# A graph layer whose first tiles come row by row from ScalarE's queue in seven groups, with a new setup order and a new end

## The chip, the cores and the metric

One NeuronCore of a Trainium2 chip runs the whole kernel. The metric is the device time of one execution in microseconds (us), the median over several executions: 2478.72 us over 9 runs, which lie between 2464.89 and 2493.82 us. The engines are named PE (TensorE; PEld is its weight load), DVE (VectorE), ACT (ScalarE), POOL (GpSimd) and SP (SyncE, which here only issues DMAs). A DMA issued by ACT is in ACT's own instruction order.

## The reference

A message-passing layer over N = 6250 nodes and E = 200000 edges, followed by a residual sum and a layer norm. The edges come sorted by destination; the sources are random.

```
w    = silu(edge_attr @ W1 + b1) @ W2 + b2              # E x 9, from E x 32
msg  = einsum('ef,em,fmg->eg', x[src], edge_sh * w, W_tp)   # F = 64, M = 9
agg  = segment_sum(msg, dst, N) / sqrt(16)
emb  = silu(node_vec[:, None] @ Wn1 + bn1) @ Wn2 + bn2
gamma, beta = split(emb, 2)
y    = layernorm(x + agg * (1 + gamma) + beta)
```

## The kernel before

**Tiling.** A tile is 128 edges, a group is KB = 16 tiles, and there are NBLK = 98 groups (the last, group 97, has 11 tiles). Because edges are sorted, all edges of a tile fall into a window of 8 consecutive nodes (a general path for other data stands behind the loop and is not taken here). The order of the instructions on each engine is the order of the code: the schedule is written out by hand, and each engine takes its instructions in that order and waits by semaphores.

**Rows of x.** Each tile needs the rows x[src], 128 x 64, in `hs`. There are three ways to get them. The first is `gather` (L89): POOL issues one indirect DMA per tile (L91) into the group's buffer of the pool `gath`, which has seven buffers; it works six groups ahead (AHEAD). The second is `pick` (L463): the last `picked(g)` tiles of a group (3 or 4, Q = 4) are selected out of a copy of x that lies in SBUF, `xs`, by one-hot matrices `hot_k`. One pick is 14 matmuls of 448 columns (seven slices h, high and low part of x) into one of two px buffers, then two DVE operations: `xm` (L484) masks the sum and L486 reduces it into `hs`. There are 355 picks. The third is `load_rows` (L98): in 16 groups (SPG: 7, 13, 19 and so on) tile 0 is not gathered; SP loads its 128 row numbers into registers, eight at a time (L101), and issues one small DMA per row (L106), 22 rows per step (SPR) over the six steps before the group's turn.

**One step of the loop (L603, i = 0 to 97)**, in order: the gathers of group i+6; the loads (`load` L367 of the edge features, `near` L378, `load_keys` L388, `gate_load` L344); `load_rows` on SP; `keys(i+2)` (L451: ACT copies the keys kr to a PSUM tile pk); the first pick of group i+1, with the matmuls of `nodes` (L582) and the first two `hots` (L456, one-hots on DVE) between its matmuls; the other hots; `hidden(i+2)` (L398: the first edge layer, then Silu on ACT into `st`, L411); `second(i+1)` (L415: the second layer, then ACT adds the bias into `p2s`, L423); `windows(i)` (L494); in odd steps `project` (L530); the second pick, with `weights` (L425: transposes of p2s and the DVE products that end in `a`, L442) and in odd steps `turn` (L548) between its matmuls; the other picks.

`windows` is the main product: for each tile a matmul (L504) of the group's hs with `a` into a tile pz, eight tiles to a pz, then four ACT copies (L514) per half into `zt`. Its first matmul waits for all gathers of the group (L509). `project` multiplies zt with W_tp (L543), and ACT copies the result to `rt` (L546). `turn` transposes it, and `halves` (L520) splits it in a high part (ACT, L524) and a low part (DVE, L525) and makes one-hots on DVE (L528). `place` (L554) adds these rows up by node (L559); ACT copies the part that goes on to the next pair (`carry`, L565), DVE adds (yt, L568), `bring` (L572) turns the sums, and `finish_nodes` (L667) does the layer norm and issues the store from SP (L684).

**Setup (L134).** SP loads src, w1 (L140), the edge features, w2 and dst; ACT's queue carries dst's first row, node_vec, b1 and then x in three parts (L155). POOL makes index vectors and begins the gathers of groups 0 to 5. DVE computes the keys of all picked rows (L209 to L217); PE transposes them, ACT copies, SP writes them to DRAM (`kd`) and `load_keys` brings them back, spread over all partitions. x is split into xs: per slice ACT copies twice (L292, L293) and DVE subtracts (L294), and `between` (L261) puts small products in between. `base` (L239) spreads dst's first row over the partitions with matmuls of one row (p_b, L242) and subtracts it (rel, L243). Then come the picks of group 0. The load of xb is issued at L318.

**End (L639 to L657).** In the last step the product of the last pair of full groups follows the picks, then windows(96) and windows(97), project, place, bring and the last store run one after the other.

The few lines that decide which tiles are gathered and picked:

```
def picked(g):                                                        # L50
    return Q - (3 * g % 8 < 3)
for t in range(g * KB + (g in SPG), g * KB + tiles(g) - picked(g))    # L94, gather
```

Of the kernel before, what the change touches and what calls it, by code (L numbers as in the profile page):

```python
# [15 lines left out]
P = 128  # L16
# [15 lines left out]
SPR = 22  # L32
EPS = 1e-5
# [16 lines left out]
def picked(g):  # L50

    return Q - (3 * g % 8 < 3)
# [7 lines left out]
def gnn_resnorm_kernel(ctx: ExitStack, tc: tile.TileContext, x, src, dst, dst_row, ea, sh, cn,  # L60
# [18 lines left out]
    with ExitStack() as fast:  # L79
# [9 lines left out]
        def gather(g):  # L89
# [4 lines left out]
                for t in range(g * KB + (g in SPG), g * KB + tiles(g) - picked(g))]  # L94

        src_r = keep.tile([len(SPG), P], I32)

        def load_rows(g, e0):  # L98
            for e in range(e0, min(e0 + SPR, P), 8):
                n = min(8, min(e0 + SPR, P) - e)  # L100
                _, vs = nc.values_load_multi_w_load_instructions(  # L101
                    src_r[SPG.index(g):SPG.index(g) + 1, e:e + n], engines=[mybir.EngineType.SP],
                    min_val=0, max_val=NPAD - 1,
                    skip_runtime_bounds_check_because="src is below N, as for the gathers")
                for k in range(n):
                    nc.sync.dma_start(hs[g][e + k:e + k + 1, 0, :], x[bass.ds(vs[k], 1), :])  # L106
# [27 lines left out]
        def setup(temp):  # L134
# [4 lines left out]
            for q in range(4):  # L139
                nc.sync.dma_start(w1bd[q * D:(q + 1) * D, (q % 2) * H:(q % 2 + 1) * H], w1)  # L140
            nc.sync.dma_start(src_i[:, AHEAD * KB:], src[:, AHEAD * KB:])
            xb_r = xb.rearrange("p j f -> p (j f)")
            row_i = xb_r[0:1, 0:NBLK * KB].bitcast(I32)
            nc.scalar.dma_start(row_i, dst[0:1, :])
            first_i = temp.tile([NBLK, KB], I32)
            nc.scalar.dma_start(first_i, dst[0].rearrange("(g k) -> g k", k=KB))
            cn_j = temp.tile([NJ, P], F32)
            nc.scalar.dma_start(cn_j, cn)
            for s in range(2):
                nc.scalar.dma_start(b1c[s * H:(s + 1) * H, :], b1.unsqueeze(1))  # L150
# [3 lines left out]
            for h0, h1 in ((0, 2), (2, 4), (4, 7)):  # L154
                nc.scalar.dma_start(xk[:, h0:h1, :], x_v[:, h0:h1, :])  # L155
            load(0)
            for s in range(2):
                nc.sync.dma_start(w2p[s * H:(s + 1) * H, s * M:(s + 1) * M], w2)
            nc.sync.dma_start(dst_i, dst)
# [14 lines left out]
            one = temp.tile([1, 1], F32)  # L174
            nc.vector.memset(one, 0.0)
            one_o = temp.tile([1, 1], F32)
            nc.scalar.activation(one_o, one, AF.Silu)
            row_f = xb_r[0:1, NBLK * KB:2 * NBLK * KB]
            nc.scalar.copy(row_f, row_i)
            first_t = temp.tile([NBLK, KB], F32)  # L180
            nc.scalar.copy(first_t, first_i)
# [5 lines left out]
            nc.vector.tensor_add(ident2, ident[:, 0:F], ident[:, F:P])  # L187
            zero = temp.tile([P, 1], F32)
            nc.vector.memset(zero, 0.0)
            for k in range(2):  # L190
                nc.vector.memset(ht[k][H:H + 1], 1.0)
            nc.vector.memset(wtc2[F:P, 4], 0.0)
            ones1 = temp.tile([1, P], F32)
            nc.vector.memset(ones1, 1.0)
            nc.vector.memset(eps, EPS)
            nc.vector.tensor_copy(nk, nk_i)
            nc.vector.tensor_copy(wi, n_i[:, 0:W])
            nc.vector.tensor_copy(li, n_i[:, 0:J])


            zt_r = zt.rearrange("p a c k w -> p (a c k w)")
            s_f, kp, kh, rest, t0, t1 = [zt_r[:, k * C:(k + 1) * C] for k in range(6)]
            ti = [t.bitcast(I32) for t in (t0, t1)]
            s_f = s_f.rearrange("p (g k) -> p g k", k=Q)
            nc.vector.tensor_copy(s_f[:, 0:NBLK - 1, :],
                                  src_i.rearrange("p (g k) -> p g k", k=KB)[:, 0:NBLK - 1, KB - Q:])
# [652 lines left out]
```

## Time and profile before

| what | value |
|---|---|
| median of 9 runs | 2478.72 us |
| the profiled execution's own time | 2489.51 us |
| its span, first to last instruction | 2487.6 us |
| mean granted TensorE clock in it | 0.818 |
| instructions | 34363 |
| bytes moved by DMA, mean rate | 96.16 MB, 39 GB/s |
| hot_k on DVE (L460) | 355, 1080 ns each, 370.3 us |
| zt copies on ACT (L514) | 784, 272 ns each, 213.6 us |
| matmuls of the picks (L475) | 4970, 409 ns each by the profile |

The profile is of one execution, taken by the hardware profiler. In a row of groups stand the source line, the engine, the operation, output<-input, the shapes, the number of instructions, and then the busy time and the mean of one; behind the second bar stand the idle time before them on their engine and what ended it ("issue": nothing the profile shows). In a row of the timeline stand the start in us, the duration, the engine, the line and the operation; x32 means that so many instructions in a row are shown together, and a bracket holds the wait before it and what ended it. SPq is the queue of SP. The waits of an engine's DMA queue are listed with the total time, the number and the longest.

### The profile page before, as it was taken

The numbers are of one execution on the slowest core, as the hardware profiler recorded it, in microseconds if no ns is written. First come the engines' busy times: TensorE is split into PE (matmuls) and PEld (weight loads), VectorE is DVE, ScalarE is ACT, GpSimd is POOL, SyncE is SP. The second block draws the span as 40 slices with busy tenths as digits, with TensorE's granted clock in tenths as the row PEclk, the third lists the DMA queues.
The fourth block names the chain that finished last, engine by engine and source line by source line (L and its number), as shares of the span: only waits on it lengthen the run. The fifth ranks groups of instructions, "written<-read, shape, count | busy, mean of one in ns | idle before, by whom it ended". The sixth has DMA issues, their size and how long they took to land.

```text
span 2487.6 us, 34363 instructions
## 1 busy us (share of the span) xinstructions
PE 1662.5 (67%) x10810; PEld 1345.6 (54%) x10810; DVE 1142.5 (46%) x1987; ACT 529.2 (21%) x1335; POOL 1128.4 (45%) x1201
## 2 busy tenths in 40 slices
PE   3077576767667577676776686667675766767697
PEld 1055464655556456555555565545564655556576
DVE  3045354544444454444544454445344535444475
ACT  2012122212122122121212121212121212212132
POOL 7634444444534454445354544544444445455400
PEclk7588787888878888888787887878888888888898
DMA  4121111111111111111111111111111111111110
GB/s 115 32 50 44 23 43 36 38 35 45 40 31 35 43 37 38 33 46 36 36 36 41 36 37 33 44 31 37 33 43 35 34 45 35 36 35 46 37 32 5
DMA packets 90940, 96.16 MB, mean 39 GB/s; under 512 B 37162, under 2 KB 51452, under 8 KB 90749
## 3 DMA queue, kind: packets, MB, share of 16 engines
q0 software_dynamic: 38144, 39.14, 8.2%
q1 hardware_dynamic: 51842, 53.09, 7.4%
q8 instruction: 88, 1.44, 0.2%
q10 hardware_dynamic: 762, 1.64, 0.2%
q14 instruction: 104, 0.84, 0.1%
HBM read 92.04 MB, written 1.73 MB: 38 GB/s over the span
## 4 chain that ended last, share of the span: by engine, by line
PE 44%; another core or an unknown queue 28%; DVE 14%; issue 11%; ACT 3%; POOL 0%; DVEq 0%; DMA 0%; POOLq 0%; ACTq 0%
PE px L475 29%; PE pz L504 4%; DVE xm L484 4%; PE p L403 3%; PE pt L543 3%; PE p L420 2%; DVE hs L486 2%; DVE a L442 2%; DVE hot_k L460 2%; PE p L430 1%; DVE c L528 1%; PE ps L559 1%; DVE p L436 1%; ACT st L411 1%
## 5 line engine op out<-in xcount | busy, mean ns | idle before, releaser
L91 POOL DMA_INDIRECT hs<-in_x_dram,src_i x1192 | 1127.1, 946 | 1244.3 <-PE pz L504 893.3
L475 PE MATMUL px<-xs,hot_k 128*128 128x448 f32 x4970 | 1264.2, 409 | 515.5 <-DVE xm L484 432.8
L475 PEld LDWEIGHTS px<-xs,hot_k 128*128 128x128 f32 x4970 | 1001.0, 212 | 648.7 <-DVE xm L484 458.3
L484 DVE SCALAR_TENSOR_TENSOR xm<-li,jl,px 128x448 f32<-128x448 f32 x355 | 240.1, 676 | 877.3 <-remote 628.5
L460 DVE TENSOR_TENSOR hot_k<-pk,nk 128x896 fp32r<-128x896 f32 x355 | 370.3, 1080 | 2.7 <-issue 2.7
L411 ACT ACTIVATE st<-p,b1c 128x1024 f32<-128x1024 f32 x98 | 109.5, 1117 | 630.3 <-PE p L403 506.6
L486 DVE TENSOR_REDUCE hs<-xm 128x64 f32<-128x448 f32 x355 | 220.0, 620 | 12.2
L514 ACT COPY zt<-pz 64x160 f32<-64x160 f32 (+2 forms) x784 | 213.6, 272 | 28.7 <-PE pz L504 20.0
L420 PE MATMUL p<-st,w2p 128*32 128x256 f32 x784 | 77.6, 445 | 164.9 <-DVE xb L356 108.7
L504 PEld LDWEIGHTS pz<-a,hs 128*64 128x64 f32 x3126 | 127.9, 160 | 49.8 <-issue 48.8
L420 PEld LDWEIGHTS p<-st,w2p 128*32 128x32 f32 x784 | 18.3, 115 | 244.1 <-issue 144.7
L504 PE MATMUL pz<-a,hs 128*64 128x72 f32 x3126 | 143.9, 255 | 0.5 <-issue 0.5
L442 DVE TENSOR_TENSOR a<-oh,p 128x1152 f32<-128x1152 f32 x98 | 132.6, 1353 | 3.3
L436 DVE TENSOR_TENSOR p<-p,sh 128x72 f32<-128x72 f32 x196 | 47.1, 240 | 173.9 <-issue 124.0
L565 ACT COPY carry<-ps 128x128 f32<-128x128 f32 x48 | 12.8, 267 | 490.5 <-PE ps L559 412.2
L403 PE MATMUL p<-ea,w1bd 64*128 64x512 f32 x392 | 114.3, 660 | 0.0
L525 DVE TENSOR_TENSOR r<-pt,r 128x128 fp32r<-128x128 f32 (+1 forms) x50 | 14.4, 288 | 165.8 <-issue 90.3
L543 PE MATMUL pt<-zt,wtc 128*64 128x128 f32 x960 | 75.9, 315 | 17.4 <-ACT st L411 15.7
L680 ACT ACTIVATE var<-var,eps 128x2 f32<-128x2 f32 (+1 forms) x25 | 7.4, 295 | 365.0 <-DVE var L679 365.0
L524 ACT CAST r<-pt 128x128 fp32r<-128x128 f32 (+1 forms) x50 | 13.2, 264 | 328.6 <-remote 247.4
L543 PEld LDWEIGHTS pt<-zt,wtc 128*64 128x64 f32 x960 | 65.6, 164 | 19.5 <-ACT st L411 17.6
L430 PE MATMUL p<-ident,p2s 128*128 128x128 f32 x196 | 54.9, 281 | 18.3 <-issue 18.2
(122 smaller groups left out, 619.9 us busy)
## 6 DMA issues: line engine op xcount, KB each, us to landing
hs<-in_x_dram SPq DMA_DIRECT2D x2048, 0.2 KB
ea<-in_ea_dram SPq DMA_DIRECT2D x49, 512.0 KB
hs<-in_x_dram,src_i POOLq DMA_INDIRECT x1192
kr<-kd SPq DMA_DIRECT2D x49, 256.0 KB
sh<-in_sh_dram SPq DMA_DIRECT2D x49, 144.0 KB
cb<-cn_d SPq DMA_DIRECT2D x12, 128.0 KB
out_dram<-o SPq DMA_DIRECT2D x24, 64.0 KB
gam<-in_x_dram ACTq DMA_DIRECT2D x2, 448.0 KB
```

The source lines that it names most:

```text
L91: hs_dma[g] = [nc.gpsimd.indirect_dma_start(out=hs[g][:, t - g * KB, :], out_offset=None, in_=x, in_offset=bass.IndirectOffsetOnAxis(ap=sr ...
L403: nc.tensor.matmul(p1[:, i, :], w1bd[i * 64:(i + 1) * 64, :], e[i * 64:(i + 1) * 64, :], start=True, stop=True)
L411: nc.scalar.activation(st[g], p1_t.pop(g), AF.Silu, bias=b1c)
L420: nc.tensor.matmul(p2[g][c * D:(c + 1) * D, 0, :].rearrange("p (i e) -> p i e", i=2), w2p, s[:, :, c * P:(c + 1) * P], start=True, stop=True)
L442: nc.vector.tensor_mul(a[g], oh_t.pop(g)[:, :, None, :].to_broadcast([P, KB, M, W]), sw.unsqueeze(3).to_broadcast([P, KB, M, W]))
L460: nc.vector.tensor_tensor(hot_k[g, t], pk_t[g][:, t, None, :].to_broadcast([P, J, P]), nk.unsqueeze(2).to_broadcast([P, J, P]), op=ALU.is_ ...
L475: nc.tensor.matmul(px.rearrange("p f l -> p (f l)"), hot_k[g, t][:, h, :], xs[i][:, h].rearrange("p f l -> p (f l)"), start=(h == 0 and i ...
L484: nc.vector.scalar_tensor_tensor(xm, li[:, None, :].to_broadcast([P, F, J]), jl[:, c:c + 1], px, op0=ALU.is_equal, op1=ALU.mult)
L486: nc.vector.tensor_reduce(hs[g][:, tiles(g) - q + t, :], xm, AX.X, ALU.add)
L504: mm = nc.tensor.matmul(pz[v * F:(v + 1) * F, k // 2].rearrange("p m w -> p (m w)"), hsg[:, k0 + k, :], ag[:, k0 + k].rearrange("p m w -> ...
L514: nc.scalar.copy(z[h * F:(h + 1) * F, 0:5 - h, k0 + v:k0 + n:2, :].rearrange("p m k w -> p k m w"), pz[v * F:(v + 1) * F, 0:(n + 1 - v) // ...
L543: nc.tensor.matmul(pt[h * F:(h + 1) * F, 0, 0:P], wtc2[:, c, :], z[h][:, c], start=(c == 0), stop=(c == 4))
```

## The change

Rows: seven groups (ACG: 16, 28 and so on to 88) get tile 0 row by row from ACT's queue, 11 rows per step (ACR) over twelve steps, into two buffers of their own (`hs_r`). The issues stand in the step after `windows`, `project` and `gate_hidden` and before the second pick. Group 97 has three picks instead of four, so there are 354 picks and 1186 gathers.

Setup: x goes first in ACT's queue, in four parts; the small loads move to SP; the keys of groups 0 and 1 are spread over the partitions by matmuls of ones with a scaled identity (`keys_first`), those of the other groups go through DRAM as before but later (`keys_rest`); x is split with one ACT copy per slice; dst's first row is spread by a broadcast DMA instead of `base`; hidden, second and weights of group 0 stand among its picks, and most of the constants come after them.

End: windows(96) comes inside step 96, ahead of the picks of group 97, project(48) and place stand among these, windows(97) takes its halves in reverse, with a px buffer beside each pz buffer, and DVE does half of its zt copies. Stores go out at the start of the next step.

```diff
@@ -30,6 +30,8 @@
 J = 7
 SPG = range(7, NBLK, 6)
 SPR = 22
+ACG = range(16, NBLK, 12)
+ACR = 11
...
-    return Q - (3 * g % 8 < 3)
+    return Q - (3 * g % 8 < 3 or g == NBLK - 1)
...
-                for t in range(g * KB + (g in SPG), g * KB + tiles(g) - picked(g))]
-        src_r = keep.tile([len(SPG), P], I32)
+                for t in range(g * KB + (g in SPG or g in ACG), g * KB + tiles(g) - picked(g))]
+        src_r = keep.tile([len(SPG) + len(ACG), P], I32)
+        row_g = list(SPG) + list(ACG)
+        hs_r = [keep.tile([P, F], F32, name=f"hs_r{k}") for k in range(2)]
         def load_rows(g, e0):
-            for e in range(e0, min(e0 + SPR, P), 8):
-                n = min(8, min(e0 + SPR, P) - e)
+            q = row_g.index(g)
+            if g in SPG:
+                eng, kind, n1, to = nc.sync, mybir.EngineType.SP, SPR, hs[g][:, 0, :]
+            else:
+                eng, kind, n1, to = nc.scalar, mybir.EngineType.Activation, ACR, hs_r[ACG.index(g) % 2]
+            for e in range(e0, min(e0 + n1, P), 8):
+                n = min(8, min(e0 + n1, P) - e)
                 _, vs = nc.values_load_multi_w_load_instructions(
-                    src_r[SPG.index(g):SPG.index(g) + 1, e:e + n], engines=[mybir.EngineType.SP],
+                    src_r[q:q + 1, e:e + n], engines=[kind],
                     min_val=0, max_val=NPAD - 1,
                     skip_runtime_bounds_check_because="src is below N, as for the gathers")
                 for k in range(n):
-                    nc.sync.dma_start(hs[g][e + k:e + k + 1, 0, :], x[bass.ds(vs[k], 1), :])
+                    eng.dma_start(to[e + k:e + k + 1, :], x[bass.ds(vs[k], 1), :])
...
             nc.sync.dma_start(src_i[:, 0:AHEAD * KB], src[:, 0:AHEAD * KB])
+            xk = gam.rearrange("p (h l) f -> p h (l f)", h=J)
+            x_v = x.rearrange("(p h l) f -> p h (l f)", h=J, l=J)
+            for h0, h1 in ((0, 1), (1, 2), (2, 4), (4, 7)):
+                nc.scalar.dma_start(xk[:, h0:h1, :], x_v[:, h0:h1, :])
             for q in range(4):
                 nc.sync.dma_start(w1bd[q * D:(q + 1) * D, (q % 2) * H:(q % 2 + 1) * H], w1)
-            nc.sync.dma_start(src_i[:, AHEAD * KB:], src[:, AHEAD * KB:])
-            xb_r = xb.rearrange("p j f -> p (j f)")
-            row_i = xb_r[0:1, 0:NBLK * KB].bitcast(I32)
-            nc.scalar.dma_start(row_i, dst[0:1, :])
-            first_i = temp.tile([NBLK, KB], I32)
-            nc.scalar.dma_start(first_i, dst[0].rearrange("(g k) -> g k", k=KB))
-            cn_j = temp.tile([NJ, P], F32)
-            nc.scalar.dma_start(cn_j, cn)
+            row_i = xb.rearrange("p j f -> p (j f)")[:, 0:NBLK * KB].bitcast(I32)
+            load(0, split=True)
+            nc.sync.dma_start(dst_i[:, 0:2 * KB], dst[:, 0:2 * KB])
+            nc.sync.dma_start(row_i[:, 0:2 * KB], rows(dst[0, 0:2 * KB], P))
             for s in range(2):
-                nc.scalar.dma_start(b1c[s * H:(s + 1) * H, :], b1.unsqueeze(1))
-            xk = gam.rearrange("p (h l) f -> p h (l f)", h=J)
-            x_v = x.rearrange("(p h l) f -> p h (l f)", h=J, l=J)
-            for h0, h1 in ((0, 2), (2, 4), (4, 7)):
-                nc.scalar.dma_start(xk[:, h0:h1, :], x_v[:, h0:h1, :])
-            load(0)
+                nc.sync.dma_start(b1c[s * H:(s + 1) * H, :], b1.unsqueeze(1))
             for s in range(2):
                 nc.sync.dma_start(w2p[s * H:(s + 1) * H, s * M:(s + 1) * M], w2)
-            nc.sync.dma_start(dst_i, dst)
+            nc.sync.dma_start(src_i[:, AHEAD * KB:], src[:, AHEAD * KB:])
+            for c in range(KB // 4):
+                q = c * D
+                nc.sync.dma_start(b2c[q:q + 2 * M, :], bass.AP(tensor=b2.tensor, offset=b2.offset,
+                                                               ap=[[0, 2], [1, M], [1, 1]]))
+            first_i = temp.tile([NBLK, KB], I32)
+            nc.sync.dma_start(first_i, dst[0].rearrange("(g k) -> g k", k=KB))
+            cn_j = temp.tile([NJ, P], F32)
+            nc.sync.dma_start(cn_j, cn)
...
+            def keys_first(g, kf, tag):
+                pk_t[g] = psum.tile([P, Q, P], F32, tag=tag, name=f"pk{g}")
+                for t in range(picked(g)):
+                    c = (g + 1) * Q - picked(g) + t
+                    d0 = NBLK * KB + c * P
+                    dg = xb.rearrange("p j f -> p (j f)")[:, d0:d0 + P]
+                    nc.vector.tensor_scalar(dg, ident, kf[:, c:c + 1], None, op0=ALU.mult)
+                    nc.tensor.matmul(pk_t[g][:, t, :], ones, dg, start=True, stop=True)
...
+            def keys_rest(kf):
+                for c0 in range(LB * Q, C, P):
+                    n = min(P, C - c0)
+                    p_kt = psum.tile([P, P], F32, tag="r", name=f"p_kt{c0}")
+                    nc.tensor.transpose(p_kt[0:n], kf[:, c0 - LB * Q:c0 - LB * Q + n], ident)
+                    kt = zt_r[:, 6 * C + c0 // 2:6 * C + c0 // 2 + P // 2].bitcast(F16)
+                    nc.scalar.copy(kt[0:n], p_kt[0:n])
+                    nc.sync.dma_start(kd[c0:c0 + n, :], kt[0:n])
+            def split(h):
+                xh = gam[:, h * J:(h + 1) * J, :].rearrange("p l f -> p f l")
+                nc.scalar.copy(xs[0][:, h], xh)
+                nc.vector.tensor_sub(xs[1][:, h], xh, xs[0][:, h].bitcast(F32))
+            kf = keys_of(0, LB)
+            keys_first(0, kf, "r")
+            hots(0, 0, 1)
+            for h in range(J):
+                split(h)
+                if h == J // 2:
+                    hots(0, 1, 2)
+            one = temp.tile([1, 1], F32)
+            nc.vector.memset(one, 0.0)
+            nc.scalar.activation(one, one, AF.Silu)
+            pick(0, 0)
+            hots(0, 2, Q)
+            keys_first(1, kf, "s")
+            hots(1, 0, 1)
+            nc.vector.tensor_copy(wi, n_i[:, 0:W])
+            nc.vector.tensor_sub(rel[:, 0:2 * KB], dst_i[:, 0:2 * KB], row_i[:, 0:2 * KB])
+            near(0)
+            pick(0, 1)
+            hots(1, 1, Q)
+            hidden(0)
+            second(0)
+            pick(0, 2, [[lambda: None, lambda: None], weights(0)])
+            hidden(1)
+            nc.sync.dma_start(dst_i[:, 2 * KB:], dst[:, 2 * KB:])
+            nc.sync.dma_start(row_i[:, 2 * KB:], rows(dst[0, 2 * KB:], P))
+            load(LB)
+            keys_rest(keys_of(LB, NBLK))
+            load_keys(LB)
...
-            def base(a_):
-                p_b = psum.tile([P, 2, KB * P // 4], F32, tag="p1", name=f"p_b{a_}")
-                for b_ in range(2):
-                    nc.tensor.matmul(p_b[:, b_, 0:NBLK * KB // 4], ones1, row_v[:, a_, b_, :], start=True, stop=True)
-                nc.vector.tensor_sub(rel_v[:, a_], dst_v[:, a_], p_b[:, :, 0:NBLK * KB // 4])
...
-            for h in range(J):
-                xh = gam[:, h * J:(h + 1) * J, :].rearrange("p l f -> p f l")
-                xp = psum.tile([P, F, J], F32, tag="px" if h in (2, 3) else "pz", name=f"x{h}", bufs=2)
-                nc.scalar.copy(xp, xh)
-                nc.scalar.copy(xs[0][:, h], xh)
-                nc.vector.tensor_sub(xs[1][:, h], xp, xs[0][:, h].bitcast(F32))
-                if h == 1:
-                    hidden_act(0)
-                between(h)
-            pick(0, 0)
-            keys(1)
-            hots(1, 0, Q)
-            base(0)
-            near(0)
-            second(0)
-            pick(0, 1)
-            base(1)
...
+            nc.vector.tensor_sub(rel[:, 2 * KB:], dst_i[:, 2 * KB:], row_i[:, 2 * KB:])
...
+        stores = []
         def finish(j0, j1, sums):
             y = late.tile([P, j1 - j0, F], F32, tag="y", name=f"y{j0}")
-            finish_nodes(nc, late, eps, sums, y, gam[:, j0:j1, :], xb[:, j0:j1, :], out_v[:, j0:j1, :], j0)
+            o = finish_nodes(nc, late, eps, sums, y, gam[:, j0:j1, :], xb[:, j0:j1, :], j0)
+            stores.append(lambda: nc.sync.dma_start(out_v[:, j0:j1, :], o))
...
+            end = g == NBLK - 1
+            for k0 in reversed(range(0, nk, ZT)) if end else range(0, nk, ZT):
...
+                pz = [psum.tile([P, ZT // 2, M, W], F32, tag="pz", name=f"pz{g}_{k0}", bufs=2)]
+                pz.append(psum.tile([P, ZT // 2, M, W], F32, tag="px", name=f"pz{g}_{k0}_", bufs=2) if end else pz[0])
...
-                                          hsg[:, k0 + k, :], ag[:, k0 + k].rearrange("p m w -> p (m w)"),
+                    mm = nc.tensor.matmul(pz[v][v * F:(v + 1) * F, k // 2].rearrange("p m w -> p (m w)"),
+                                          hs_r[ACG.index(g) % 2] if g in ACG and k0 + k == 0 else hsg[:, k0 + k, :],
+                                          ag[:, k0 + k].rearrange("p m w -> p (m w)"),
...
-                        nc.scalar.copy(
+                        (nc.vector.tensor_copy if end and v else nc.scalar.copy)(
                             z[h * F:(h + 1) * F, 0:5 - h, k0 + v:k0 + n:2, :].rearrange("p m k w -> p k m w"),
-                            pz[v * F:(v + 1) * F, 0:(n + 1 - v) // 2, h:M:2, :])
+                            pz[v][v * F:(v + 1) * F, 0:(n + 1 - v) // 2, h:M:2, :])
...
+                while stores:
+                    stores.pop(0)()
...
-                if i < NBLK - 2:
+                if i < NBLK - 1:
                     windows(i)
-                turn = project(i // 2) if i % 2 == 1 else []
+                turn = project(i // 2) if i % 2 == 1 and i < NBLK - 1 else []
                 if i % 4 == 1 and i - 1 < NJ:
                     gate_hidden(i - 1)
+                for g in ACG:
+                    if 0 < g - i <= 2 * AHEAD:
+                        load_rows(g, (2 * AHEAD - g + i) * ACR)
                 if i + 1 < NBLK:
                     pick(i + 1, 1, [weights(i + 1), turn])
+                if i == NBLK - 2:
+                    sums(i + 1)
+                    turn = project(i // 2)
+                    ps = psum.tile([P, 2 * P], F32, tag="s", name="ps_l")
+                    pick(i + 1, 2, [turn])
+                    more = place(i // 2, ps)
+                    if picked(i + 1) < Q:
+                        for f in more:
+                            f()
+                        more = []
+                    pick(i + 1, 3, [more])
+                    continue
...
-                if i == NBLK - 1:
-                    for f in turn:
-                        f()
-                    ps = psum.tile([P, 4, P], F32, tag="s", name="ps_l")
-                    for f in place(i // 2, ps[:, 0:2].rearrange("p a n -> p (a n)")):
-                        f()
-                    py = psum.tile([P, FB, F], F32, tag="r", name="py_l")
-                    for f in bring(NJ - 3, NJ - 1, py):
-                        f()
-                if i >= NBLK - 2:
-                    windows(i)
-                if i == NBLK - 2:
-                    sums(i + 1)
+            for f in bring(NJ - 3, NJ - 1, psum.tile([P, FB, F], F32, tag="s", name="py_l")):
+                f()
+            windows(NBLK - 1)
             project(NBLK // 2)
-            ps = psum.tile([P, 4, P], F32, tag="s", name="ps_n")
-            for f in place(NBLK // 2, ps[:, 0:2].rearrange("p a n -> p (a n)")):
+            ps = psum.tile([P, 2 * P], F32, tag="p1", name="ps_n")
+            for f in place(NBLK // 2, ps) + bring(NJ - 1, NJ, psum.tile([P, 1, F], F32, tag="r", name="py_n")):
                 f()
-            for f in bring(NJ - 1, NJ, psum.tile([P, 1, F], F32, tag="r", name="py_n")):
-                f()
+            while stores:
+                stores.pop(0)()
```

## The prediction

> **What bounds the kernel now.** I read, in this order, the page's busy shares and groups, the waits, and the timeline of three stretches: one pair of steps in the middle, the setup, and the last steps. No engine is full: TensorE (PE) is busy 67%, GpSimd (POOL) 45%. The page's groups and the waits:
>
> ```profile
> PE 1662.5 (67%) x10810; PEld 1345.6 (54%) x10810; DVE 1142.5 (46%) x1987; ACT 529.2 (21%) x1335; POOL 1128.4 (45%) x1201
> L91 POOL DMA_INDIRECT hs<-in_x_dram,src_i x1192 | 1127.1, 946 | 1244.3 <-PE pz L504 893.3
> L484 DVE SCALAR_TENSOR_TENSOR xm<-li,jl,px 128x448 f32<-128x448 f32 x355 | 240.1, 676 | 877.3 <-remote 628.5
> SPq L106 <- DMA hs<-in_x_dram: 29.2, 51, 1.2
> ```
>
> POOL waits 893 us for PE to release gather buffers, so the gathers are not late. DVE waits 628 us for something "remote" before it reads a pick's sum. The timeline shows what that is. Around 1200 us (gathers running), and in the last steps (none left):
>
> ```profile
> 1214.92 0.67 PE L475 MATMUL px<-xs,hot_k 128*128 128x448 f32 x2
> 1215.43 0.27 ACT L546 COPY rt<-pt 128x128 f32<-128x128 f32 x1 [1.02 <-PE pt L543]
> 1222.61 0.27 ACT L524 CAST r<-pt 128x128 fp32r<-128x128 f32 x1 [6.91 <-PE px L475]
> 1227.09 0.95 POOL L91 DMA_INDIRECT hs<-in_x_dram,src_i  x1 [0.30 <-issue]
> 1228.96 0.68 DVE L484 SCALAR_TENSOR_TENSOR xm<-li,jl,px 128x448 f32<-128x448 f32 x1 [5.25 <-remote]
> ...
> 2397.54 1.22 PE L504 MATMUL pz<-a,hs 128*64 128x72 f32 x32
> 2398.10 11.29 SPq L106 DMA_DIRECT2D hs<-in_x_dram  x22
> 2402.05 0.68 DVE L484 SCALAR_TENSOR_TENSOR xm<-li,jl,px 128x448 f32<-128x448 f32 x1
> 2404.85 0.68 DVE L484 SCALAR_TENSOR_TENSOR xm<-li,jl,px 128x448 f32<-128x448 f32 x1 [1.47 <-PE px L475]
> 2411.97 1.22 PE L504 MATMUL pz<-a,hs 128*64 128x72 f32 x32
> ```
>
> A pick is 14 matmuls. Without gathers one ends every 2.80 us (2402.05 to 2404.85), although SP issues 22 rows in the same time. With gathers, the pick that began at 1214.92 gave its sum only at 1228.96, just after the last gather of its burst: "remote" is PE itself, and it crawls while POOL gathers. Steps tell the same: between the windows of groups 4 and 88 (240.2 to 2318.9 us) a step takes 2078.7 / 84 = 24.7 us with 12.2 gathers; between those of 92 and 95 (2397.54 to 2439.93) it takes 42.4 / 3 = 14.1 us with none. So a gather costs (24.7 - 14.1) / 12.2 = 0.87 us of the path, against a pitch of 0.95 + 0.30 = 1.25 us. The setup is the same crawl:
>
> ```profile
> 37.94 0.68 DVE L484 SCALAR_TENSOR_TENSOR xm<-li,jl,px 128x448 f32<-128x448 f32 x1 [6.90 <-remote]
> 49.13 0.97 DVE L243 TENSOR_TENSOR rel<-dst_i,p_b 128x784 f32<-128x784 int32 x1 [5.87 <-remote]
> 70.83 0.47 ACT L423 ACTIVATE p2s<-p,b2c 128x256 f32<-128x256 f32 x1 [39.97 <-issue]
> 110.03 0.68 DVE L484 SCALAR_TENSOR_TENSOR xm<-li,jl,px 128x448 f32<-128x448 f32 x1 [59.47 <-remote]
> 138.59 1.22 PE L504 MATMUL pz<-a,hs 128*64 128x72 f32 x32
> ```
>
> From 37.94 to 110.03 us PE finishes 4 + 8 + 14 matmul records and as many weight loads (an fp32 matmul stands as two records): 72.1 / 52 = 1.39 us a record. SP is idle then, so gathers alone do it. The stream of 87 gathers (groups 0 to 6) ends at 111.8, and the first windows start at 138.59.
>
> **The change, part by part.**
>
> Setup. ACT's two copies per slice of x (926 + 955 ns) become one, and DVE subtracts straight from gam; x is first in ACT's queue (four DMAs instead of three, ahead of nothing else). The first two groups' keys no longer go through DRAM (kr was waited for until 21.1); they are 3 + 4 fp32 matmuls on scaled identities. The two base products (8 records each in loads and matmuls) are gone, replaced by a broadcast DMA of dst, and SP no longer stands at L318 from 37.9 to 119.8. All the small loads move to SP: some 20 issues at 0.42 us (rows of L140) before 12 us, against 8 for x on ACT. PE's list before the first windows stays about as long, so what counts is how much is done before the crawl. It begins near 24 us: SP's issues of b2c take 0.31 us up to 21 us and about 0.7 us from 32 us. The first pick now waits for x's first slices: issued at 0.75 us instead of 3.93, first used at 14.03 before, so it runs from somewhere between 7 and 14 us instead of 25.3. After its end (7 casts of 0.95 us later) PE has, up to the first windows, 184 records to do: pick 28, keys 16, hidden 8, second 16, pick with transposes 36, hidden 8, three small products and the key transposes 20, pick 28, hidden 8, second 16. By 24 us between none and 104 of them are done, in the crawl (111.8 - 24) / 1.39 = 63 more, so 17 to 121 are left at 111.8; at 0.1 us each (2.80 / 28) with some 5 us of waits for DVE the windows start at about 114 to 129 us. Gain 10 to 25, I take **18 us**, the middle: nothing in the trace places x's landing. The gain holds only if the chain of the third group's keys (DVE, PE, ACT, SP, DRAM, SP) is through by then; if not, part is lost.
>
> End. Before, windows 96 starts at 2461.45, after four picks, and everything up to windows 97 (2469.72) is serial. Now windows 96 follows the second product of group 97 (ended 2452.33): 1.2 us, then pick 1 and transposes 3.4, project 1.4, pick 2 with the turn 2.9, its xm and reduce 1.3: windows 97 can start at 2462.6, 7.1 earlier, of which 2.8 is the pick left out. Its zt copies (1.95 us on ACT, after a square root) are shared with DVE: 1 to 2 us more. One last store issue of 0.4 us waits for the end. Gain 4 to 10, I take **8 us**: the chain above has few unknowns.
>
> Gathers. Seven leave, one comes for the pick left out: 6 x 0.87 = **5 us**; bounds 0 (POOL waits anyway) and 6 x 1.25 = 7.5. The rows' own transfers cost PE nothing, by the 22 rows beside full-speed picks above.
>
> A rule speaks against this part: the Trainium skill, "DMA: Bandwidth & Descriptors", section "Issuing engines are not separate DMA queues", says that DMAs from several engines share the same 16 DMA engines, and that spreading them saves only issue time. By it these 5 us would be 0, and the sum 5 us later; the row above, PE's 2.80 us beside 22 SP rows and its crawl beside gathers, says that the issuing queue does matter here, and I go by it.
>
> ACT's rows. In 84 steps (4 to 87) ACT gets 11 issues, with the address arithmetic before each, and two loads of registers, behind the zt copies (and rt), ahead of r, the next pk, carry, st and p2s. Priced as SP's: 0.41 to 0.51 us a row outside bursts (11.29 / 22), loads about 1 us: 11 x 0.41 + 2 = 6.5 us. In the odd step shown rt ends at 1215.70, so ACT is free at 1222.2, and r is released at 1222.61. What is queued behind: DVE's subtraction of r stands ahead of the xm at 1228.96; with r 0.27, r's low half 0.29 and two hots 0.60, ACT may take until 1228.0, a run of 12.3 us, before anyone is late. In the even step zt ends at 1243.33 and pk is wanted by DVE only after the xm at 1260.21. There is a second wait: DMAs of SP and ACT use the same eight semaphores in turn, and each waits for the landing of the one eight before (51 such waits of SP, 29.2 us). SP now runs up to a step ahead; it will be held to ACT's rows, and ACT's rows to SP's. From no cost to 20 us over the loop, if rows keep SP's fast pace; I take **9 us** lost, nearer the low end because SP is ahead of PE through most of the loop. At SP's pace in the late part of a burst it is more, see the first rival.
>
> Stores. Each goes one step later, so SP no longer stands at L684 for DVE (83.5 + 68.2 us). SP is covered by being ahead: 0 either way; if SP were late, this is what would help.
>
> **Sum.** -18 - 8 - 5 + 9 = -22 us. The profiled execution took 2489.5 us (span 2487.6 and 1.9 around it): 2467.5. It lies 10.8 us over the median of the runs, 2478.7, so the median becomes **2457 us**.
>
> **Rivals.** (1) *ACT's rows hold up DVE: slower.* SP's rows late in a burst are dear: the 14 from 1213.39 take 15.53 us, the last six about 1.4 us each or more. Were ACT's eleven 1.36 us each, the run is 11 x 1.36 + 2 = 17 us, 4.7 past the 12.3; PE has a second px buffer, so about half of it in 42 odd steps counts: 99 us instead of 9, time 2547. It decides from 12.3 + 31 / 42 = 13.0 us, that is 1.0 us a row. For it: row pace in bursts. Against: ACT's own instructions keep their pace in bursts (zt copies 0.27), its rows begin at the burst's start, where SP's first eight took 4.1 us, and that is a run near 11. (2) *The setup is timed by the gather stream all the same:* x lands late, or the third group's keys do, and the windows stay near 138. The 18 us go: 2475. For it: 87 gathers end at 111.8 whatever is done; against: 27 us lie between that and the windows. (3) *Gathers are free after all* (POOL's 893 us): 2462, within the forecast's own range.
>
> **Chances.** Forecast with (3) 0.67, its own range 2437 to 2466; setup gain lost 0.14; slower 0.19. About 0.5%, 12 us, is what a measurement can tell from no change. Faster 0.67, same 0.14, slower 0.19. The range, 2434 to 2505, leaves out the slow tail and little below.
>
> **What would show it.** First windows at 114 to 129 us; windows 97 to end unchanged but for 1 to 2 us; steps 24.6 us in the loop, where ACT's eleven issues fit in 12 us; POOL with 1186 gathers; no new wait of DVE r L525 for ACT r over 5 us. I am wrong if loop steps grow: then look at DVE's wait for ACT, and at ACT's and SP's waits for each other's landings.

## The result, and the profile after

The changed kernel takes 2585.73 us (median of 10 runs, 2578.34 to 2595.43) against 2478.72 us: a ratio of 1.0465, interval 1.0435 to 1.0494. It is slower; a gain of 22 us was forecast. Its profiled execution has a span of 2583.4 us, 95.8 us more than before. By the first matmuls of `windows` in the two traces these split up so:

| stretch | before, us | after, us | difference |
|---|---|---|---|
| start to windows 4 | 240.2 | 229.7 | -10.5 |
| windows 4 to 88, the steps with ACT's rows | 2078.7 | 2185.2 | +106.5 |
| windows 88 to 95 | 121.0 | 127.1 | +6.1 |
| windows 95 to the end | 47.7 | 41.4 | -6.3 |

Setup and end gained, 16.8 us together; the loop lost. Three views of the profile after. First the page's busy shares and groups:

```profile
PE 1651.3 (64%) x10801; PEld 1339.8 (52%) x10801; DVE 1141.8 (44%) x2005; ACT 524.2 (20%) x1321; POOL 1122.8 (43%) x1195
L93 POOL DMA_INDIRECT hs<-in_x_dram,src_i x1186 | 1121.5, 946 | 1353.5 <-PE pz L519 1001.8
L495 DVE SCALAR_TENSOR_TENSOR xm<-li,jl,px 128x448 f32<-128x448 f32 x354 | 239.2, 676 | 714.9 <-remote 477.3
L541 DVE TENSOR_TENSOR r<-pt,r 128x128 fp32r<-128x128 f32 x48 | 13.9, 290 | 426.8 <-ACT r L540 219.7
```

No engine's counted busy time grew; register instructions and the issuing of DMAs, which is what ACT now does more of, are not in it. POOL waits 109 us longer for PE to release its buffers (1001.8 against 893.3). DVE now idles 426.8 us ahead of the low part of r (L541, L525 before), where it was 165.8 us. The waits (engine, line, what for: us in total, times, longest):

```profile
ACT pk L465 <- issue: 344.2, 48, 15.4
DVE r L541 <- ACT r L540: 222.6, 22, 14.2
...
DVE p L447 <- remote: 51.5, 2, 48.2
...
PE p_kt L236 <- DVE zt L218: 44.5, 1, 44.5
```

The second is the wait I named as what would show me wrong: DVE's r for ACT's r, 14.2 us at the longest. The last two belong to the setup. The timeline of one odd step (windows 41 at 1204.7 us):

```profile
1207.87 0.27 ACT L563 COPY rt<-pt 128x128 f32<-128x128 f32 x1
1209.26 0.27 PE L566 MATMUL pt<-ident,rt 128*128 128x128 f32 x1
1209.67 11.40 ACTq L116 DMA_DIRECT2D hs_r<-in_x_dram  x10
1222.05 0.27 ACT L540 CAST r<-pt 128x128 fp32r<-128x128 f32 x1 [13.20 <-issue]
1222.34 0.29 DVE L541 TENSOR_TENSOR r<-pt,r 128x128 fp32r<-128x128 f32 x1 [12.13 <-issue]
1223.07 0.68 DVE L495 SCALAR_TENSOR_TENSOR xm<-li,jl,px 128x448 f32<-128x448 f32 x1
1223.81 4.96 PE L486 MATMUL px<-xs,hot_k 128*128 128x448 f32 x16 [10.67 <-DVE c L544]
```

ACT issues rows from 1209.67 to 1221.07, r comes at 1222.05, behind it on DVE stand r's low part and xm, and PE stands 10.67 us for a px buffer, which xm frees. A cut from these rows, instruction by instruction from the trace, from the sixth row on (start us, duration ns; FUSED_REGOPS and MOVE work out an address in registers, TENSOR_LOAD loads row numbers):

```
1211.794   29 MOVE          1214.727    5 DMA
1211.863  228 DMA           1214.745  171 TENSOR_LOAD
1212.120   37 FUSED_REGOPS  1215.454  691 FUSED_REGOPS
1212.185  328 MOVE          1216.855    3 MOVE
1213.289   10 DMA           1217.540   14 DMA
1213.311    3 FUSED_REGOPS  1218.245  708 FUSED_REGOPS
1214.014  700 MOVE          1218.958  712 MOVE
                            1220.370  700 DMA
```

Six rows go out, about 0.39 us apart; then most instructions, a register move too, take about 0.70 us or start 0.70 us after the one before. The gathers began at 1206.17. Over the loop 11 rows take 12.2 us. Single times among these are not exact: in 25 cases over the 42 odd steps (here too, at 1223.87) the record of a row stands behind the start of r, which comes after it in the code.

### The profile page after: what moved, and what is told of

The parts are those of the page before. It is cut to its first block, busy times and chain, and to the rows that moved or that the text cites. A ratio compares the mean times of both kernels' runs of the same rounds, so it can differ in the third digit from the quotient of the medians.

```text
span 2583.4 us, 37215 instructions
## 1 busy us (share of the span) xinstructions
PE 1651.3 (64%) x10801; PEld 1339.8 (52%) x10801; DVE 1141.8 (44%) x2005; ACT 524.2 (20%) x1321; POOL 1122.8 (43%) x1195
## 4 chain that ended last, share of the span: by engine, by line
PE 30%; issue 15%; another core or an unknown queue 12%; DVE 9%; ACTq 5%; ACT 3%; SPq 1%; DMA 1%; DVEq 0%
PE px L486 21%; ACTq L116 4%; DVE xm L495 2%; PE pz L519 2%; PE p L414 2%; PE pt L560 2%; DVE hs L497 1%; DVE a L453 1%; PE p L431 1%; SPq L116 1%; ACTq L111 1%; ACT zt L530 1%; ACT st L422 1%; DVE hot_k L471 1%
## 5 line engine op out<-in xcount | busy, mean ns | idle before, releaser
L93 POOL DMA_INDIRECT hs<-in_x_dram,src_i x1186 | 1121.5, 946 | 1353.5 <-PE pz L519 1001.8
L497 DVE TENSOR_REDUCE hs<-xm 128x64 f32<-128x448 f32 x354 | 219.4, 620 | 12.3
L530 ACT COPY zt<-pz 64x160 f32<-64x160 f32 (+1 forms) x780 | 212.0, 272 | 13.2 <-PE pz L519 4.5
L541 DVE TENSOR_TENSOR r<-pt,r 128x128 fp32r<-128x128 f32 x48 | 13.9, 290 | 426.8 <-ACT r L540 219.7
L465 ACT CAST pk<-kr 128x512 f32<-128x512 f16 (+1 forms) x96 | 52.7, 549 | 477.4 <-issue 344.2
L431 PE MATMUL p<-st,w2p 128*32 128x256 f32 x784 | 69.7, 430 | 118.2 <-DVE xb L363 66.4
L519 PEld LDWEIGHTS pz<-a,hs 128*64 128x64 f32 x3102 | 118.5, 150 | 46.3 <-issue 45.3
L519 PE MATMUL pz<-a,hs 128*64 128x72 f32 x3102 | 134.1, 244 | 3.1 <-issue 2.3
L447 DVE TENSOR_TENSOR p<-p,sh 128x72 f32<-128x72 f32 x196 | 47.1, 240 | 184.6 <-issue 54.6
L414 PE MATMUL p<-ea,w1bd 64*128 64x512 f32 x392 | 115.9, 658 | 13.4 <-DMA ea<-in_ea_dram 11.2
L540 ACT CAST r<-pt 128x128 fp32r<-128x128 f32 x48 | 12.7, 265 | 537.8 <-issue 225.8
L560 PEld LDWEIGHTS pt<-zt,wtc 128*64 128x64 f32 x960 | 60.7, 155 | 15.4 <-ACT st L422 15.1
L441 PE MATMUL p<-ident,p2s 128*128 128x128 f32 x196 | 54.9, 280 | 14.6 <-issue 14.6
```

The source lines that it names most:

```text
L93: hs_dma[g] = [nc.gpsimd.indirect_dma_start(out=hs[g][:, t - g * KB, :], out_offset=None, in_=x, in_offset=bass.IndirectOffsetOnAxis(ap=sr ...
L414: nc.tensor.matmul(p1[:, i, :], w1bd[i * 64:(i + 1) * 64, :], e[i * 64:(i + 1) * 64, :], start=True, stop=True)
L497: nc.vector.tensor_reduce(hs[g][:, tiles(g) - q + t, :], xm, AX.X, ALU.add)
L519: mm = nc.tensor.matmul(pz[v][v * F:(v + 1) * F, k // 2].rearrange("p m w -> p (m w)"), hs_r[ACG.index(g) % 2] if g in ACG and k0 + k == 0 ...
L530: (nc.vector.tensor_copy if end and v else nc.scalar.copy)(z[h * F:(h + 1) * F, 0:5 - h, k0 + v:k0 + n:2, :].rearrange("p m k w -> p k m w ...
L560: nc.tensor.matmul(pt[h * F:(h + 1) * F, 0, 0:P], wtc2[:, c, :], z[h][:, c], start=(c == 0), stop=(c == 4))
```

## The experiments

Three theories. **T1**: what is queued behind the rows on ACT (r, pk) is late. **T2**: while gathers run, instructions are scarce for all engines, and ACT's additional ones make PE later. **T3**: the DMAs themselves, by their landings and the semaphores shared with SP.

The runs fell on two kinds of chips, which differ more than the kernels do: on the first kind the kernel before takes 2479 to 2521 us, on the second 1521 to 1524 us. All ratios are to the kernel before on the same chip, and conclusions are kept apart by kind.

| kernel | kind | us | ratio, interval | odd / even step, us |
|---|---|---|---|---|
| before | first | 2478.7 | | 26.9 / 22.6 |
| the change | first | 2585.7 | 1.0465 (1.0435 to 1.0494) | 27.8 / 24.3 |
| no ACT rows | first | 2504.6 | 0.9967 (0.9926 to 1.0008) | 27.2 / 23.0 |
| rows only | first | 2662.4 | 1.0563 (1.0491 to 1.0635) | 28.9 / 24.9 |
| fixed rows | first | 2599.5 | 1.0339 (1.0264 to 1.0413) | 27.1 / 25.1 |
| 35 short copies | first | 2708.4 | 1.0762 (1.0685 to 1.0838) | 29.8 / 25.2 |
| new end, 11 short copies | first | 2628.0 | 1.0458 (1.0364 to 1.0553) | 27.8 / 24.7 |
| fixed rows, early loads | first | 2625.8 | 1.0456 (1.0368 to 1.0544) | 27.4 / 25.5 |
| the change | second | 1721.5 | 1.1319 (1.1300 to 1.1338) | 20.1 / 14.6 |
| no ACT rows | second | 1526.3 | 1.0018 (1.0008 to 1.0028) | 15.0 / 14.9 |
| 11 short copies | second | 1524.2 | 1.0018 (1.0009 to 1.0028) | 15.1 / 14.8 |
| 11 long copies | second | 1949.1 | 1.2810 (1.2789 to 1.2832) | 25.1 / 15.2 |
| rows behind r | second | 1692.6 | 1.1124 (1.1100 to 1.1149) | 18.9 / 15.2 |
| fixed rows | second | 1588.0 | 1.0425 (1.0406 to 1.0443) | 16.8 / 14.9 |
| no rows at all | second | 1543.0 | 1.0142 (1.0125 to 1.0159) | 15.1 / 15.2 |
| rows in even steps | second | 1522.5 | 0.9991 (0.9981 to 1.0001) | 15.0 / 14.8 |

(A step is counted from windows i to windows i+1, mean over i = 4 to 87; odd and even by i. The runs of the first kind come from more than one chip; steps of the kernel before were traced on the first of these only, so its steps compare with those of the change. "No ACT rows" to "35 short copies" share a chip and compare with each other.)

**Which part loses.** Without ACT's rows:

```diff
-ACG = range(16, NBLK, 12)
+ACG = range(0)
```

> The changed kernel without ACT's rows: the seven first tiles are gathered again; setup, end and stores stay as changed. If the rows on ACT are the whole loss, what is left is the gain of setup and end seen in the two traces (about 10 us by the windows of group 4, 6 us from the windows of group 95 on): 2479 - 16 = about 2463 us, 2455 to 2472. If the new setup or the deferred stores slow the loop, it stays over 2500 us.

The rows alone (load_rows, gather and windows of the change in the kernel before):

> The kernel before with ACT's rows and nothing else of the change. If the rows are the whole loss: 2479 + 107 + 16 = about 2600 us, 2585 to 2615. If rows and new setup or stores only hurt together: near 2480 to 2540 us.

The first gives 0.9967, the second 1.0563: the rows are the whole loss, and it needs nothing else of the change. What setup, end and stores gain together can't be told from nothing here (interval to 1.0008).

**Length, number or DMAs.** The rows from a fixed address, 11 instructions a step:

```diff
+            if g in ACG:
+                for e in range(e0, min(e0 + n1, P)):
+                    eng.dma_start(to[e:e + 1, :], x[e:e + 1, :])
+                return
```

> The changed kernel, with ACT's 896 row loads kept, but from a fixed address (row e of x in place of row src[e], so the result of these tiles differs): 11 instructions per step in place of some 35, with the same number of DMAs, bytes and landings. T1, ACT's run delays what is queued behind it: the run falls to 5 to 8 us, under the 12.3 us of cover, so 2465 to 2480 us. T2, while gathers run each instruction an engine has to get costs about 0.7 us and ACT's take from PE: a third of the loss stays, about 2500 us (2490 to 2515). T3, it is the DMAs themselves (landings, the semaphores shared with SP): 2570 to 2590 us.

35 one-element copies in place of the rows, no DMA:

```diff
-                for g in ACG:
-                    if 0 < g - i <= 2 * AHEAD:
-                        load_rows(g, (2 * AHEAD - g + i) * ACR)
+                if 4 <= i <= 87:
+                    for k in range(35):
+                        nc.scalar.copy(junk[:, 1:2], junk[:, 0:1])
```

> The changed kernel without ACT's rows (the tiles are gathered), but with 35 copies of one element on ACT in the same place of the same 84 steps: instructions without DMAs. T1: they take 35 x 0.2 = 7 us where ACT gets instructions at full pace, under the cover: 2465 to 2475 us; at 0.7 us each they run 24 us and it is over 2600 us. T2: as many instructions as the rows, so about the same loss: 2560 to 2600 us. T3: no DMA, no loss: 2460 to 2470 us.

The fixed rows hold ACT only 3.7 us and r comes 9.9 us after windows, sooner than before (12.4), yet 1.0339 stays: T1 is not the whole. The copies lose more (1.0762) without a DMA: T3 isn't needed, though here r is late too (19.1 us after windows), since the 35 copies hold ACT 14.0 us, so that T1 can have a part. In the fixed rows the waits speak for T3:

```profile
SPq L120 <- DMA hs_r<-in_x_dram: 97.2, 35, 7.4
PE p L418 <- DMA ea<-in_ea_dram: 82.4, 19, 7.6
```

SP stands at landings of ACT's rows, so the edge features come late and PE waits 82 us for them, as much as this run is slower (82 us). In the change itself PE waits only 11.2 us for edge features, and with the rows alone 0.3 us. Two more runs on the first kind of chip: the loads a step earlier, and 11 short copies (2.4 us of ACT, no DMA) on the kernel before with the new end.

```diff
                 if i % LB == 1 and i + 1 + LB < NBLK:
+                    load(i + 1 + LB)
                     load_keys(i + 1 + LB)
```

> The fixed rows again, with the loads of edge features issued one step earlier on SP. In both runs of the fixed rows PE waited 73 to 82 us for these loads, because SP stood at landings of ACT's rows. If that is what the fixed rows cost (T3): on a chip of about 1520 us 1.0425 falls to 0.995 to 1.012, on one of about 2480 to 2520 us 1.034 falls to 0.99 to 1.01. If it is ACT's instructions (T2), the ratio stays at 1.03 to 1.04.

> The kernel before with the new end (and three picks in group 97) alone, plus the 11 one-element copies on ACT per step. On a chip of about 1520 us, where the copies cost 0.1%: there POOL's stream of gathers sets the time up to group 97, so the end is worth little: one gather more (1.25 us) against a shorter tail, ratio 0.995 to 1.002. On a chip of about 2480 to 2520 us: T2, instructions on ACT alone hold up PE: 1.02 to 1.035; else 0.993 to 1.003.

With early loads PE no longer waits for edge features, and the ratio is 1.0456, over what either theory expected. But the run doesn't speak against T3, for another wait took the place of the first:

```profile
SPq L120 <- DMA hs_r<-in_x_dram: 126.3, 34, 8.3
PE pz L523 <- DMA hs<-in_x_dram: 97.1, 15, 12.3
```

SP still stands at landings of ACT's rows, and now its own rows come late: in the loop PE waits for them ahead of windows 7, 13, 19 and so on, the groups whose first tile SP loads. The 97 us are nearly all of the 105 us lost. So landings can be the whole loss of the fixed rows, twice; they are not that of the change, where PE's waits for DMAs sum to 11.5 us.

Eleven tiny copies alone give 1.0458, more than T2 expected, and without any DMA. The timeline of this run, an even and an odd step:

```profile
1202.02 0.68 PE L477 MATMUL px<-xs,hot_k 128*128 128x448 f32 x2
1202.56 0.65 PE L477 MATMUL px<-xs,hot_k 128*128 128x448 f32 x2
1203.08 8.08 PE L477 MATMUL px<-xs,hot_k 128*128 128x448 f32 x38
1205.42 0.68 DVE L486 SCALAR_TENSOR_TENSOR xm<-li,jl,px 128x448 f32<-128x448 f32 x1
1219.49 0.68 DVE L486 SCALAR_TENSOR_TENSOR xm<-li,jl,px 128x448 f32<-128x448 f32 x1 [12.73 <-remote]
...
1231.83 2.39 ACT L643 COPY junk<-junk 1x1 f32<-1x1 f32 x11
1232.36 0.27 PE L555 MATMUL pt<-ident,rt 128*128 128x128 f32 x1
1242.84 0.27 ACT L529 CAST r<-pt 128x128 fp32r<-128x128 f32 x1 [8.62 <-issue]
1243.14 0.29 DVE L530 TENSOR_TENSOR r<-pt,r 128x128 fp32r<-128x128 f32 x1 [6.22 <-issue]
1244.25 0.95 POOL L91 DMA_INDIRECT hs<-in_x_dram,src_i  x1 [0.30 <-issue]
```

In the even step PE's 42 matmuls are three picks of 14, at full pace by their records. The second pick's last one starts at 1207.91, but DVE is idle until 1219.49. The update of PE's semaphore that DVE waits for is in the trace, at 1219.47: the signal is late, not DVE. In the odd step the copies end at 1234.22 and r's input, by PE's record, at 1232.63, and r runs at 1242.84. The trace shows no release for this one, but in 39 of the loop's 42 odd steps of this run r starts at an update of PE's semaphore. So ACT is not short of its own next instruction there; it waits for PE's signal.

This lateness is what the runs share. From the start of a pick's last matmul to DVE's xm, taking the second xm of the even steps, there pass 5.5 us in the kernel before and 5.9 without ACT's rows, but 8.8 in the change and 8.9 here. By PE's records this pick isn't held up by anything behind ACT's rows or copies, so T1 doesn't explain it. That ACT's additional instructions cost is shown; that they do it by holding up PE fits these numbers, but how much of the loss it makes is not shown (the fixed rows have 8.9 us as well, and 6.2 with early loads), nor whether PE's matmuls run late or only its signals. The cost isn't in proportion: 11 copies lose about as much as 11 rows with some 35 instructions.

**The second kind of chip.** The 11 short copies and the 11 long ones (junk then is 128 x 840), which tell T1 from T2, and the change itself:

```diff
-                        nc.scalar.copy(junk[:, 1:2], junk[:, 0:1])
+                        nc.scalar.copy(junk, xs[0].rearrange("p h f l -> p (h f l)")[:, 0:840].bitcast(F32))
```

> The changed kernel without ACT's rows, with 11 one-element copies on ACT in their place in each of the 84 steps: as many instructions as the 11 fixed rows, but no DMA and some 2.5 us of ACT. T2, the number of instructions: like the fixed rows, ratio 1.02 to 1.035. T3, the DMAs: no loss, 0.995 to 1.005.

> As the 11 one-element copies, but each of 840 elements (about 0.95 us), so that ACT is held some 10.5 us, as by the rows at 0.95 us each, with the same 11 instructions. T1, what is queued behind ACT: clearly over the short copies, ratio 1.03 to 1.05. T2 alone: the same as the short copies within 0.5%.

> The changed kernel once more, so that the runs sent with it have it on their own chip. On a chip where the kernel before takes about 2480 to 2520 us: ratio 1.04 to 1.05. On one where it takes about 1520 us (gathers do not slow the other engines there): the rows fit into 5 to 7 us at 0.39 us each, r is some 6 us later and PE and DVE are near full, ratio 1.01 to 1.06.

Here the short copies cost nothing (1.0018, as without ACT's rows), so T2 isn't seen on these chips. As many copies that hold ACT 10.1 us cost 28%, nearly all in odd steps: T1 alone, and far more than the 3% to 5% expected. The change loses 13%, more than expected, and in odd steps only:

```profile
802.00 6.50 ACTq L116 DMA_DIRECT2D hs_r<-in_x_dram  x11
808.54 0.27 ACT L540 CAST r<-pt 128x128 fp32r<-128x128 f32 x1 [7.74 <-DMA hs<-in_x_dram]
808.84 0.29 DVE L541 TENSOR_TENSOR r<-pt,r 128x128 fp32r<-128x128 f32 x1 [5.42 <-ACT r L540]
810.30 6.16 PE L486 MATMUL px<-xs,hot_k 128*128 128x448 f32 x16 [4.43 <-DVE xm L495]
```

The rows take only 6.5 us, but nothing on PE or DVE is slow enough to hide it: without ACT's rows r comes 5.2 us after windows on this kind, with them 10.3. Two ways out: the rows behind r in ACT's order (the same three lines after the last pick), and the rows in even steps only, for three groups over 24 steps:

```diff
-                    if 0 < g - i <= 2 * AHEAD:
-                        load_rows(g, (2 * AHEAD - g + i) * ACR)
+                    if i % 2 == 0 and 0 < g - i <= 4 * AHEAD:
+                        load_rows(g, (4 * AHEAD - g + i) // 2 * ACR)
```

> The changed kernel with ACT's rows at the end of the step's code, behind r (the high part) and ahead of the next pk, in place of between rt and r. T1, r late behind the rows: the odd steps get back what they lost, the ratio to the kernel before falls from 1.0465 to 1.00 to 1.02. T2, instructions that ACT gets while gathers run hold up PE's: no matter where they stand, 1.035 to 1.06.

> The changed kernel with ACT's 11 rows in even steps only, over 24 steps, for three groups (28, 52, 76). r stands in odd steps, so T1 has nothing to hold up. On a chip of about 1520 us: no loss, three gathers fewer than without rows: 0.2% under that run. On one of about 2480 to 2520 us: T1 as without rows (0.995 to 1.000); T2 or T3, the even steps are some 1.9 us longer, 36 x 1.9 = 68 us: 1.02 to 1.03.

With the rows behind it, r is in time (5.1 us after windows), and the ratio is still 1.1124, a miss for both answers:

```profile
SPq L116 <- DMA hs_r<-in_x_dram: 239.8, 90, 7.6
PE p L414 <- DMA ea<-in_ea_dram: 131.1, 34, 6.6
```

PE's 131 us are most of the 171 us lost. In the change SP waits nearly as long at these landings on this kind (218.8 us), but PE only 1.1 us for edge features. So another place alone doesn't cure it; the waits speak for T3, which no run isolates here. The fixed rows on this kind:

> The rows from a fixed address again (11 instructions, no register loads). On a chip of about 1520 us: ACT's run falls from 6.5 us and 3 us of register loads to about 4 us, so r is nearly in time: T1 gives 1.00 to 1.03, where the change has 1.13; if landings shared with SP are the cost, 1.08 or more. On a chip of about 2480 to 2520 us: 1.034 again.

1.0425 lies between the two answers: r is in time (5.9 us), and PE waits 73 us for edge features, about the loss of 62 us against the run without ACT's rows. T3 is only argued here, since the early loads weren't run on this kind.

In even steps the rows are free: 0.9991 against 1.0018 without them, and the medians differ by 3.7 us for three gathers saved, 1.25 us each being 3.75. This is the best version there, level with the kernel before; it was not run on the first kind.

Last, neither ACT's nor SP's rows:

> The changed kernel without ACT's rows and without SP's rows either: all first tiles are gathered, 16 more gathers than the run without ACT's rows (ratio 0.997). By my 0.87 us a gather it is 14 us slower: ratio 1.000 to 1.005. T2 with SP included (SP issues 22 rows of three instructions in a step): PE gets its instructions sooner in every step, ratio 0.95 to 0.985.

16 more gathers cost 1.0142 / 1.0018 = 1.2%, 1.2 us each: on the second kind POOL's stream sets the time. Whether SP's 22 rows a step also hold up PE on the first kind wasn't tried there. Three kernels ran again on another chip of the second kind, with the same results: short copies 1.0022, 1.0018 and 1.0025, long ones 1.2810 and 1.2814, no rows 1.0142 twice.

## Why the prediction was wrong

- **ACT's rows, +9 us: the step that failed.** By the runs they cost 1.0465 / 0.9967 = 5.0%, about 124 us (the two ratios are of different chips), and 5.6% alone. The term put at nothing what ACT's additional instructions do to the other engines while gathers run. Even steps, in which nobody was to be late, lost 1.7 us each, odd ones 0.8 (42 of each: some 71 and 35 of the loop's 106.5 us), and 11 copies without a DMA cost 4.6%. The price of a run was too low as well: 12.2 us, not 6.5, as the last rows come at 0.70 us an instruction.
- **The cover of 12.3 us** (12.1 by its own rows: 1228.96 less 1.16 is 1227.8) was read off r's wait for PE. That wait is real, but it is not slack of the kernel:

```profile
1217.28 0.27 PE L549 MATMUL pt<-ident,rt 128*128 128x128 f32 x1
...
ACT r L524 <- remote: 247.4, 27, 13.2
```

The record of r's input ends at 1217.55; the update of PE's semaphore comes at 1222.59 and r at 1222.61. In 41 of the loop's 42 odd steps before, r starts at such an update, on average 6.3 us after the record of its input; on the second kind of chip it is 0.04 us. What I took for cover is PE's own lateness under the gathers. On the first kind it did hide most of the run (the odd steps lost the less), though r then came 17.0 us after windows instead of 12.4 and at PE's signal in only 5 of 42 odd steps; on the second there is none of it, and the rows cost 13%.
- **"ACT's own instructions keep their pace in bursts."** The first in a burst do (six rows, 11 copies, zt); of what comes later many take 0.70 us, and 35 copies of 0.19 us took 14.0 us. I had this number twice, as SP's late rows and as PE's 1.39 us a record in the setup (2 x 0.70), and read it as two facts on two engines; that it is one fact is likely but not shown.
- **"PE itself, and it crawls"** is half right. PE's signal is late: 99 of the 101 idle times over 3 us ahead of xm in the loop before end at an update of PE's semaphore. But its matmul records in the loop stand at full pace (the pick that began at 1214.92 starts its last one at 1217.99), so a slow pace of the matmuls is not what the trace shows there.
- **Rival 1** had the sign and nearly the size (99 us, 2547), partly by luck: its mechanism, odd steps late behind ACT, is what the second kind of chip shows. On the first kind odd steps gave only some 35 us, and the even steps lost more, which neither it nor the forecast had.
- **The wait by the shared semaphores** was right as named: SP waited 44.8 us for ACT's rows, but PE only 11.2 us for edge features. It mattered in the fixed rows, and by the waits in the rows behind r.
- **Setup, -18 us (10 to 25):** 10.5 us by windows 4, inside its bounds, but the first windows began at 132.9, not 114 to 129. That sign was a poor one: with the same setup they began at 99.0 in the run without ACT's rows, and windows 4 came no earlier for it (228.7 against 229.7). The stated condition failed too: PE stood 44.5 us, to 104.0, for the third group's keys, whose chain on DVE stood behind a wait of 48.2 us at L447, where DVE takes PE's transposes.
- **End, -8 us (4 to 10):** 6.3 us from windows 95 on. Right in size; all of it came ahead of windows 97, from which the end took 17.9 us before and 18.0 after, so the 1 to 2 us for shared zt copies did not come.
- **Gathers, -5 us:** on the second kind 1.2 us a gather, the pitch, near the upper bound; on the first not separable.
- **The rule I set aside**, of the Trainium skill ("DMA: Bandwidth & Descriptors", "Issuing engines are not separate DMA queues"), that another queue saves issue time only: the prediction took it to make the 5 us nothing, but a gather's pitch of 1.25 us on POOL is issue time. The rows in even steps saved 3.7 us for three gathers, 3.75 us of POOL's issue, so on the second kind the runs agree with the rule. On the first, copies without any DMA cost as much as the rows, and no run decides it.

## What to carry to other kernels

Before idle time is counted as cover, look at what ends it: here it was another engine's late signal, which is part of the problem and not room to spare. Work moved to a half-idle in-order queue is paid for by what is queued behind it: place it where the next instruction's consumer is far off (even steps, here). When a wait is taken away, look for the one that replaces it before a theory is dropped (the early loads, here). And measure on more than one chip before a gain of a per cent is believed.

## What the hardware showed unexpectedly

The same program took 2479 to 2521 us on some chips and 1521 to 1524 us on others, at a gather pitch of 1.25 us on both. In the change's own loop 11.8% of the 5355 register instructions (MOVE and FUSED_REGOPS) of SP and ACT took 0.6 to 0.8 us on the first kind; on the second none of 5372 did. From the start of a pick's last matmul to DVE's xm (second xm of the even steps, without ACT's rows) it was 5.9 us on the first and 0.40 us on the second. The mean granted clock was 0.81 on the first and 0.98 on the second (without ACT's rows). What makes the difference is open.
